# Seven block products (Strassen) for the projections of a delta-rule layer in batches two to four

## The chip, the core and the metric

The kernel runs on one core of a Trainium2 chip. The time is device microseconds of one execution: 3435.01 us is the median of three runs (3433.98 to 3443.59).

## What is computed

A decoder layer in float32 on x of 4 sequences by 512 tokens by 512 channels. Three blocks follow each other, each added to x: a gated delta-rule attention, a cross attention, and an ordinary attention with a mixture of experts. The change touches the first. It has 16 heads with keys and values of 128 channels:

```python
q = _causal_conv(x @ Wq.T, cw_q, cb_q)      # 4 taps, then SiLU
k = _causal_conv(x @ Wk.T, cw_k, cb_k)
v = _causal_conv(x @ Wv.T, cw_v, cb_v)
g = exp(-exp(A_log) * softplus(x @ Wa.T + dt_bias)); beta = sigmoid(x @ Wb.T)
q, k = l2norm(q), l2norm(k)
# per token t and head: S is a 128 x 128 state
error = v_t - g_t * (S k_t)
S = g_t * S + k_t (beta_t * error)^T
o_t = S^T q_t
o = rmsnorm(o) * norm_w * silu(x @ Wg.T)
return o @ Wo.T
```

## The kernel before

**Tiling.** Tokens of a sequence are worked in four chunks of 128 (TB = 4). A *pair* m is two neighbouring heads of one sequence: b = m // 8 is the sequence (called batch), hg = m % 8 the two heads; there are 32 pairs. Four projections belong to a pair, numbered n = 0 (q), 1 (k), 2 (v), 3 (gate g); one projection of one pair, 256 outputs by 512 channels by 512 tokens, is called a *unit* here. `conv` (L569 to L593) makes half a unit, one head: four matmuls of 128x128 weights by 512 tokens into a PSUM bank (L578; in the trace each float32 matmul counts as two passes), then for g a SiLU from PSUM, else the convolution: a scaled copy on ACT (L586), three multiply-adds on DVE that read the projection from PSUM (L589), and a SiLU on ACT (L592). The weights of a unit (512 KB) are loaded by `load_weights` into one buffer for each n, once its last user is done.

**Stages of a pair.** `stage1(m)` makes k for both heads, its transposes (L621) and their copy (L623), the sums of squares (ACT L626, clipped on DVE L632), their inverse roots by a power on POOL (L633), and from these the factors `ee` (L635), `ke` and `nr`; then the decay matrices `em`, spread by a scan on DVE (L642) and scaled by `ee` on ACT (`scale`, L438, four instructions per head), the k-k products (L651), then q, its product with k (`product`, 666), the decayed keys (`decayed`) and the sums of q's squares (`pss`, L698). `stage2_inverse(m)` inverts 32x32 diagonal blocks on POOL (L731, L732) and sends them through DRAM as T and X. `stage2_values(m)` makes v, transposes it (L779), multiplies it by `nr` (DVE, L781), and makes the gate. `stage3(m)` joins the blocks to full inverses (py L827 and L850, px L837 and L859, copies on ACT), and then runs the recurrence over the four chunks: for each head r (matmul L879, DVE L881), u (matmul L888, ACT L890), the new state (matmul L898, DVE L903) and the outputs into two banks `po` (L906, L908). `output(m)` multiplies by Wo (L952) and adds into the rows of x on DVE (L957).

**Order.** The stages are Python generators. `turns` mixes them: for each step of `stage3(m)` two steps of `stage1(m + 2)`, one of `stage2_values(m + 1)`, one of the inversion and one of `output(m - 1)`. ACT, DVE and POOL execute in exactly this written order (`manual_schedule`); for PE and for SP, which issues most transfers, a scheduler chooses the order when the kernel is built. Each engine then executes in order: an instruction that waits holds all behind it on its engine. A DMA that SP issues waits in SP's queue until its buffer is free.

**PSUM.** Eight banks of 128x512: four called `pb` (`p_b`) for everything wide, two called `ps` (`p_s`), each holding one 128x128 result of the recurrence at a time, two called `po`.

Of the kernel before, what the change touches and what calls it, by code (L numbers as in the profile page):

```python
# [31 lines left out]
F32 = mybir.dt.float32  # L32
BF16 = mybir.dt.bfloat16
AF = mybir.ActivationFunctionType
ALU = mybir.AluOpType
# [27 lines left out]
C_UP, C_LO, C_ONE, C_ID4, C_INV, N_TAB_A = 0, 1, 2, 3, 7, 7 + 8 // GRP  # L63
# [3 lines left out]
def _tables():  # L67
    ta, t = np.zeros((P, N_TAB_A, P), np.float32), np.zeros((P, N_TAB, P), np.float32)
    r, c = np.arange(P)[:, None], np.arange(P)[None, :]
    t[:, C_ID] = r == c  # L70
    ta[:, C_UP] = r <= c
    ta[:, C_LO] = r > c
    ta[:, C_ONE] = 1.0


    eye = np.eye(32, dtype=np.float32).reshape(32, 32 // GRP, GRP).transpose(2, 0, 1)
    ta[: GRP * 32, C_INV : C_INV + 8 // GRP] = eye.repeat(32, axis=0).reshape(GRP * 32, 8 // GRP, P)
    ta[:, C_ID4 : C_ID4 + 4] = (r == c)[:, None, :]
    t[:, C_CAUSAL] = np.where(c <= r, 0.0, MASKED)
    inv = (np.float32(1.0) / np.float32(1e6) ** (np.arange(0, RD, 2, dtype=np.float32) / np.float32(RD))).astype(np.float32)  # L80
    ang = (np.arange(S, dtype=np.float32)[:, None] * inv[None, :]).astype(np.float32)
    cos, sin = np.cos(ang), np.sin(ang)
    rope = np.concatenate([cos, cos, -sin, sin], axis=1).reshape(TB, P, P)
    t[:, C_ROPE : C_ROPE + TB] = rope.transpose(1, 0, 2)
    t[:, C_RANK, :NE] = np.arange(NE, 0, -1)
    t[:, C_RANK, NE : 2 * NE] = np.arange(NE) * B * S
    t[:, C_RANK, 16 : 16 + NT] = c[:, :NT] * P + r
    t[:, C_RANK, 32:96] = np.arange(64)
    t[:, C_BEFORE] = r < c
    t[:, C_ONES] = 1.0  # L90

    n = NE * (B * S + P) // P
    rows = np.zeros((P, n, 2), np.float32)
    rows[:, :, 0] = B * S + (np.arange(P * n) % P).reshape(P, n)
    t[:, C_LIST:].reshape(P, -1)[:, : 2 * n] = rows.reshape(P, 2 * n)
    return ta, t
# [8 lines left out]
def decoder(ctx: ExitStack, tc: tile.TileContext, a: dict, out: bass.AP):  # L105
# [21 lines left out]
    def rsqrt(dst, src, pool, add=0.0, mul=1.0):  # L127

        n = src.shape[1]
        t = pool.tile([P, 64], F32, name="rsq")  # L130
        nc.vector.tensor_scalar(t[:, :n], src, mul, add, ALU.mult, ALU.add)  # L131
        nc.gpsimd.tensor_tensor(dst, t[:, :n], mhalf[:, :n], ALU.pow)  # L132
# [233 lines left out]
    with ExitStack() as st:  # L366
# [10 lines left out]
        p_b = st.enter_context(tc.tile_pool(name="a_pb", bufs=4, space=PSUM))  # L377
        p_s = st.enter_context(tc.tile_pool(name="a_ps", bufs=2, space=PSUM))
        p_o = st.enter_context(tc.tile_pool(name="a_po", bufs=1, space=PSUM))

        tab_a = keep.tile([P, C_INV, P], F32, name="tab_a")
        nc.scalar.dma_start(tab_a, a["a_tables"][:, 0:C_INV, :])
        id4 = tab_a[:, C_ID4 : C_ID4 + 4, :].rearrange("p a b -> p (a b)")
# [21 lines left out]
        r_d = [dram.tile([HG * TB, P], F32, name=f"r_d{n}") for n in range(SLOTS)]  # L405

# [25 lines left out]
        def chunks(t):  # L432
            return t.rearrange("p c j -> p (c j)")
# [15 lines left out]
        def prologue(b):  # L449
# [18 lines left out]
            for c in range(TB):  # L468
                t = x[c]
                run(norms_of[c])  # L470
                if b:
                    yield
                    if c + 1 < TB:
                        next(norms_of[c + 1])
                    yield
                if c == 0:
                    xnT = s2.tile([P, KD, S], F32, name="xnT", bufs=2)
                    seqs[b] = [xnT]
                tp = p_b.tile([P, KD, P], F32, name="pb")
                for kd in range(KD):  # L480
                    nc.tensor.transpose(tp[:, kd, :], t[:, kd * P : (kd + 1) * P], ident)
                nc.scalar.copy(xnT[:, :, c * P : (c + 1) * P], tp)
                if b > 0 and c + 2 < TB:
                    load(c + 2)
                    norms_of.append(layernorm(x[c + 2].unsqueeze(1), x[c + 2].unsqueeze(1), small))
                yield
# [6 lines left out]
            yield  # L493
            pab = p_b.tile([P, TB, 32], F32, name="pb")
            for c in range(TB):
                nc.tensor.matmul(pab[:, c, :], quarters[:, c * P : (c + 1) * P], fold, start=True, stop=True)
            g_a, lg, beta, gam, ngam, gend, gall = (seq.tile([P, H1, TB], F32, name=n) for n in ("g_a", "lg", "beta", "gam", "ngam", "gend", "gall"))
# [63 lines left out]

        weights = {}

        def load_weights(m, *what, by=nc.sync):

            for n in what:
                if m < B * NHG:
                    t = (s1 if n < 2 else s2).tile([P, KD, HG * P], F32, name=f"w{n}", bufs=1)
                    by.dma_start(t, a["a_w"][m % NHG][:, n])  # L569
                    weights[m, n] = t  # L570
# [24 lines left out]
        keys, pairs = {}, {}  # L595

        def stage1(m):
# [3 lines left out]
            wk, wq = weights.pop((m, 1)), weights.pop((m, 0))  # L601

            def rows(n):
                t = s1.tile([P, HG, S], F32, name=f"row{n}", bufs=1)
                nc.sync.dma_start(chunks(t), g_d[b, n, hg * HG * TB : (hg + 1) * HG * TB].rearrange("c t -> (c t)").partition_broadcast(P))
                return [t[:, p, :] for p in range(HG)]

            kT, kt = [], []
            ss = small.tile([P, HG * TB], F32, name="ss", bufs=2)
            for p in range(HG):  # L610
                t = live.tile([P, S], F32, name="kT")
                yield from conv(b, hg, p, 1, wk, t)
                kT.append(t)
                yield
            xnT, beta, gam, ngam, gend, gall = seqs[b]
            gb = rows(0)
            load_weights(m + 1, 1)
# [21 lines left out]
            for p in range(HG):  # L639

                e = s1.tile([P, TB, P], F32, name="em")
                nc.vector.tensor_tensor_scan(chunks(e), gb[p], id4, 0.0, ALU.mult, ALU.add)  # L642
                em.append(e)
                yield
# [15 lines left out]
            qh, qg, pt, sq, kd_ = [], [], [], [], []  # L660

            def product(p):
# [4 lines left out]
                t = live.tile([P, TB, P], F32, name="pt", bufs=6)  # L667
                nc.vector.tensor_tensor(t, pq, em[p], ALU.mult)
                pt.append(t)

# [5 lines left out]
            for p in range(HG):  # L676
                q = s1.tile([P, S], F32, name="qh")
                c = conv(b, hg, p, 0, wq, q)
                yield from itertools.islice(c, 2)
                if p:  # L680
                    product(0)
                yield from c
                qh.append(q)
                g = live.tile([P, S], F32, name="qg", bufs=6)
                nc.gpsimd.tensor_tensor(g, q, mb[p], ALU.mult)  # L685
                qg.append(g)
                t = w2.tile([P, S], F32, name="cv", bufs=5)
                nc.scalar.activation(t, q, AF.Square)
                sq.append(t)
                yield  # L690
            load_weights(m + 1, 0)
            decayed(0)
            yield
# [11 lines left out]
            yield  # L705
            product(1)
# [3 lines left out]
            keys[m] = (kT, kd_, qg, pt, nr, rq)  # L710
# [57 lines left out]
        def stage2_values(m):  # L768
# [3 lines left out]
            wv, wg = weights.pop((m, 2)), weights.pop((m, 3))  # L772
            v_, gs = [], []
            for p in range(HG):
                t = yield from conv(b, hg, p, 2, wv, None)
                yield
                tp = p_b.tile([P, TB, P], F32, name="pb")
                for c in range(TB):
                    nc.tensor.transpose(tp[:, c, :], t[:, c * P : (c + 1) * P], ident)  # L779
                v = w2.tile([P, TB, P], F32, name="vn", bufs=4)  # L780
                nc.vector.tensor_tensor(v, tp, along(nr[:, p * TB : (p + 1) * TB], P), ALU.mult)  # L781
                v_.append(v)
# [5 lines left out]
            load_weights(m + 1, 2)  # L788
            for p in range(HG):
                g = w2.tile([P, S], F32, name="gs", bufs=3)  # L790
                yield from conv(b, hg, p, 3, wg, g)
                gs.append(g)
            load_weights(m + 1, 3)
# [19 lines left out]
        def stage3(m):  # L813
# [56 lines left out]
            for c in range(TB):  # L870
                cs = slice(c * P, (c + 1) * P)
                rs = []
                for p in range(HG):
# [4 lines left out]
                    pk = p_s.tile([P, P], F32, name="ps")  # L878
# [7 lines left out]
                for p in range(HG):  # L886
                    pu = p_s.tile([P, P], F32, name="ps")
# [6 lines left out]
                for p in range(HG):  # L894
                    h = hg * HG + p
                    if c < TB - 1:
                        pn = p_s.tile([P, P], F32, name="ps")
# [81 lines left out]
        def prepare():  # L979
# [4 lines left out]
            wk = [live.tile([P, S], F32, name="qg", bufs=6) for _ in range(2)]  # L984
            wk += [chunks(live.tile([P, TB, P], F32, name="pt", bufs=6)) for _ in range(2)]
# [66 lines left out]
        load_weights(0, 1, 0, 2, 3, by=nc.scalar)  # L1052
# [6 lines left out]
        run(itertools.islice(start, TB + 1))  # L1059
        pair0 = stage1(0)  # L1060
# [5 lines left out]
        for m in range(NP):  # L1066
            rest, turn = [], [0]
            if m == NP - 2:
# [5 lines left out]
                x_kT = x_keep.tile([P, 3, KD, M], BF16, name="x_kT")  # L1074
                nc.sync.dma_start(x_kT, x_kT_d)
# [3 lines left out]
            if m == NP - 1:  # L1079
                second.close()  # L1080
                v_keep = top.enter_context(tc.tile_pool(name="v_keep", bufs=1, side="right", reuse_waits="tile"))
                wpj = v_keep.tile([P, KD, D], F32, name="wpj")
# [22 lines left out]
            rest = turns(*rest)  # L1105
            for _ in stage3(m):
                next(rest, None)
            turn.clear()
# [631 lines left out]
```

## Time and profile before

| | |
|---|---|
| median of three runs | 3435.01 us (3433.98 to 3443.59) |
| profiled execution | 3435.95 us |
| its span | 3434.2 us |
| mean granted clock of TensorE | 0.978 |
| delta stage | 0 to some 1880 us |
| POOL power L633 | 32 times, 2438 ns each |
| DVE addition of 128x256 from PSUM (L1297) | 424 ns |
| DVE addition of 128x512 from PSUM (L957) | 689 ns |
| POOL multiplication of 128x512 (L685) | 1283 ns |

PE is TensorE's matmul queue, PEld its weight loads, which run beside it, DVE VectorE, ACT ScalarE, POOL GpSimd, SP the engine that issues DMAs. A group's row names line, engine, operation, output and inputs, shapes and count, and then busy time, mean nanoseconds of one instruction, and the idle time of the engine just before such instructions with what ended it. Matmuls are pipelined, so the mean of one (0.603 us for 512 columns) is longer than the distance from one to the next. A timeline row gives start and length in microseconds of a run of equal instructions, and in brackets the wait before it and what it waited for. Windows give the busy time of each engine in a stretch of the span. The granted clock is the share of full speed that TensorE was allowed.

### The profile page before, as it was taken

Reading aid. Unit: us, or ns where it says so; the run is one execution under the profiler, and the core shown is the slowest. Engines: PE = TensorE matmul, PEld = TensorE weight load, DVE = VectorE, ACT = ScalarE, POOL = GpSimd, SP = SyncE. Lnnn points to the kernel's source line nnn. Section 1 sums busy time; section 2 is a strip of 40 time slices with the busy share of each in tenths; the row PEclk is TensorE's granted clock in tenths of the full one; section 3 lists DMA queues with packets and bytes.
Section 4 is the critical chain, followed back from the end, with each engine's and each line's share of the span. In section 5 each row is a group of like instructions: output and inputs, shape, how many; then the busy total and the mean of one; then the engine's idle time right before and its main releaser. Section 6 shows DMA issues by size and latency. Waiting matters only on the chain. (4 is left out here: it accounts for less than half of the span.)

```text
span 3434.2 us, 49083 instructions
## 1 busy us (share of the span) xinstructions
PE 3253.7 (95%) x16596; PEld 1815.8 (53%) x16596; DVE 1836.7 (53%) x4155; ACT 1600.1 (47%) x4336; POOL 1449.6 (42%) x2766
## 2 busy tenths in 40 slices
PE   5899999999999999999997899999999999999996
PEld 2455555555555555555554455555555545554443
DVE  5755565555645556555545566656655665655111
ACT  3445555455554555455534345455454545534121
POOL 1156766667566675766752211121112111212442
PEclk7999999999999999999998899999999999999998
DMA  6343434534445343453432654445445544546444
GB/s 172 111 124 110 135 110 123 162 110 130 112 122 157 117 134 110 123 151 114 131 103 68 226 181 158 144 159 186 152 142 164 167 153 145 159 165 221 90 83 95
DMA packets 462250, 473.97 MB, mean 138 GB/s; under 512 B 199199, under 2 KB 310821, under 8 KB 461808
## 3 DMA queue, kind: packets, MB, share of 16 engines
q1 hardware_dynamic: 448656, 440.66, 42.2%
q0 software_dynamic: 11904, 27.34, 3.9%
q8 instruction: 132, 2.16, 0.3%
q10 hardware_dynamic: 1440, 2.84, 0.3%
q14 instruction: 118, 0.97, 0.1%
HBM read 410.15 MB, written 64.81 MB: 138 GB/s over the span
## 5 line engine op out<-in xcount | busy, mean ns | idle before, releaser
L578 PE MATMUL pb<-xnT,w 128*128 128x512 f32 x2048 | 959.4, 603 | 0.1
L578 PEld LDWEIGHTS pb<-xnT,w 128*128 128x128 f32 x2048 | 364.3, 192 | 337.4 <-issue 330.9
L589 DVE SCALAR_TENSOR_TENSOR cv<-pb,pp,cv 128x510 f32<-128x510 f32 (+2 forms) x576 | 424.3, 746 | 99.0 <-ACT cv L586 85.7
L732 POOL TENSOR_TENSOR iT<-iT,iW 64x126 f32<-64x126 f32 (+22 forms) x930 | 345.6, 372 | 72.8
L1229 PE MATMUL pb<-c_q,hT 128*128 128x512 f32 x768 | 362.9, 611 | 2.9 <-DMA c_q<-in_c_wk_dram 2.7
L731 POOL TENSOR_TENSOR iW<-iA,iT 64x126 f32<-64x126 f32 (+22 forms) x930 | 320.2, 344 | 65.8 <-issue 0.2
L952 PE MATMUL pb<-wot,og 128*128 128x512 f32 x512 | 246.0, 604 | 6.4 <-DVE xa L957 4.3
L1153 POOL TENSOR_TENSOR rope_s<-q,tab 128x128 f32<-128x128 f32 x64 | 36.6, 572 | 461.2 <-DVE q L1259 403.4
L1229 PEld LDWEIGHTS pb<-c_q,hT 128*128 128x128 f32 x768 | 144.6, 197 | 157.2 <-issue 153.5
L586 ACT ACTIVATE cv<-pb,pp 128x512 f32<-128x512 f32 x192 | 148.7, 774 | 147.5 <-PE pb L578 143.6
L633 POOL TENSOR_TENSOR rk<-ss,mhalf 128x8 f32<-128x8 f32 x32 | 78.0, 2438 | 277.3 <-DVE ss L632 277.3
L957 DVE TENSOR_TENSOR xa<-pb,xa 128x512 f32<-128x512 f32 x112 | 77.1, 689 | 189.8 <-PE pb L952 189.7
L1325 PE MATMUL po<-eT,val 128*128 128x512 f32 x320 | 167.2, 619 | 11.6 <-ACT eT L1323 8.6
L295 ACT ACTIVATE x_e<-pb,nm,x_step 128x256 f32<-128x256 f32 x256 | 141.2, 563 | 75.5 <-DVE nm L291 68.0
L1295 PE MATMUL pb<-kT,qT 128*128 128x256 f32 (+3 forms) x576 | 166.5, 416 | 0.7 <-ACT og L1301 0.6
L1335 PE MATMUL pw<-wot,oT 128*128 128x512 f32 x344 | 163.5, 602 | 0.4 <-DVE oT L1327 0.2
L685 POOL TENSOR_TENSOR qg<-qh,row 128x512 f32<-128x512 f32 x64 | 82.1, 1283 | 176.7 <-ACT qh L592 153.9
L952 PEld LDWEIGHTS pb<-wot,og 128*128 128x128 f32 x512 | 92.2, 191 | 101.8 <-issue 88.9
L1630 PE MATMUL pb<-w_gu,eT 128*128 x312 | 142.1, 599 | 2.0 <-issue 2.0
L1323 ACT COPY eT<-pb 128x512 f32<-128x512 f32 x160 | 90.8, 594 | 107.1 <-PE pb L1321 106.8
L592 ACT ACTIVATE qh<-cv 128x512 f32<-128x512 f32 x64 | 40.3, 630 | 213.0 <-DVE cv L589 205.1
L132 POOL TENSOR_TENSOR rms_r<-rsq,mhalf 128x1 f32<-128x1 f32 x48 | 27.4, 571 | 245.1 <-DVE rsq L131 245.0
(390 smaller groups left out, 6216.6 us busy)
## 6 DMA issues: line engine op xcount, KB each, us to landing
c_q<-in_c_wq_dram SPq DMA_DIRECT2D x128, 512.0 KB
w<-in_a_w_dram SPq DMA_DIRECT2D x124, 512.0 KB
wot<-in_c_wo_dram SPq DMA_DIRECT2D x86, 512.0 KB
row<-g_d SPq DMA_DIRECT2D x64, 512.0 KB
c_o<-in_c_wo_dram SPq DMA_DIRECT2D x42, 512.0 KB
at_d<-at SPq DMA_DIRECT2D x64, 256.0 KB
T<-t_d SPq DMA_DIRECT2D x32, 512.0 KB
X<-x_d SPq DMA_DIRECT2D x32, 512.0 KB
```

Source lines behind the costliest of these rows:

```text
L295: nc.scalar.activation(e[:, 2 * r + g, :], ps[r][:, g, :], AF.Exp, bias=nm[:, r, g : g + 1], scale=step[:, h : h + 1], accum_out=ssum[:, g ...
L578: nc.tensor.matmul(pj, wt[:, kd, p * P : (p + 1) * P], xnT[:, kd, :], start=kd == 0, stop=kd == KD - 1)
L586: nc.scalar.activation(ac, pj, AF.Identity, bias=cb[:, m, h : h + 1], scale=cw[:, m, h, 3:4])
L589: nc.vector.scalar_tensor_tensor(ac[:, j:], pj[:, : S - j], cw[:, m, h, 3 - j : 4 - j], ac[:, j:], ALU.mult, ALU.add)
L731: eng.tensor_tensor(u, A[:, i, i + 1 :].unsqueeze(2).to_broadcast([nb, n, w]), T[:, i, :w].unsqueeze(1).to_broadcast([nb, n, w]), ALU.mult)
L732: eng.tensor_tensor(T[:, i + 1 :, :w], T[:, i + 1 :, :w], u, ALU.add)
L952: nc.tensor.matmul(pw, og[p][:, c * P : (c + 1) * P], wot[:, p, :], start=p == 0, stop=p == HG - 1)
L1229: nc.tensor.matmul(pj, hT[:, kd, :], w[:, kd % 2, :], start=kd == 0, stop=kd == KD - 1)
L1295: nc.tensor.matmul(ps[:, m, k * P : (k + w) * P], qT[g][:, n + m, :], kT[:, g, j : j + w, :], start=True, stop=True)
L1325: nc.tensor.matmul(po, val[:, g, :], eT, start=k == 0, stop=k == c)
L1335: nc.tensor.matmul(pw, oT[:, h + m, :], w[:, m, :], start=g == 0 and h + m == 0, stop=g == 3 and h + m == 3)
L1630: nc.tensor.matmul(pg, hT[:, kd, :], w_gu[:, bass.ds(e, 1), kd, :, :], start=kd == 0, stop=kd == KD - 1)
```

## The change

For pairs of the first sequence (m < 8) a unit is projected as before. From m = 8 on it is made as a 2x2 block product by Strassen's method in the form with seven products: halves of the outputs (the two heads), of the channels and of the tokens. A product is two matmuls of 128x128 weights by 256 tokens, so 14 of 256 columns stand in place of 8 of 512. Their results are added on DVE into SBUF (`plus`), and the convolution then reads SBUF. A unit is now finished for both heads before its convolution begins (`seven`, `convs`).

```diff
+        def seven(b, n, wt, dst):
+            x = moving[b]
+            def products(*ns):
+                ps = p_b.tile([P, 2, S // 2], F32, name="pb")
+                for k, n in enumerate(ns):
+                    w, v = x[n]
+                    for kd in range(2):
+                        nc.tensor.matmul(ps[:, k], wt[:, w, kd, :], v[:, kd, :], start=kd == 0, stop=kd == 1)
+                return ps[:, 0], ps[:, 1]
...
+            l, r = products(0, 4)
+            nc.scalar.copy(c11, l)
+            plus(c12, c11, r)
+            yield
+            l, r = products(5, 2)
+            plus(c21, c12, l)
+            plus(c22, c21, r)
+            plus(c12, c12, r)
+            yield
+            l, r = products(1, 3)
+            plus(c11, c11, l)
+            plus(c21, c21, r)
+            yield
+            l, _ = products(6)
+            plus(c12, c12, l)
+            yield
```

The four sums of weight blocks that a unit needs are made once, while the first sequence uses the same weights plainly (`combine`: four additions of 128x256, on POOL for the first six units, on DVE for the rest), stored to DRAM (`used`), and read back with the plain blocks by the later sequences (`load`). Weight buffers are now three in turn for all units, filled three units ahead. The sums of x's blocks are four subtractions on POOL per sequence (`differences`).

```diff
+        def combine(u):
+            if u[0] < NHG:
+                t = summed[u] = s1.tile([P, 3, 2, S // 2], F32, name="xd", bufs=1)...
+                eng = nc.gpsimd if u in order[:6] else nc.vector
+                for dst, x, y, op in ((t3, a11, a21, ALU.subtract), ...):
+                    eng.tensor_tensor(dst, x, y, op)
...
+            if m < NHG:
+                nc.sync.dma_start(sums_d[m % NHG, n], summed.pop((m, n)))
+            if i + 1 < len(order):
+                combine(order[i + 1])
+            weights.pop((m, n))
+            load()
```

PSUM is divided anew: five banks for `pb`, one for the recurrence, whose four quarters are used in turn.

```diff
-        p_b = st.enter_context(tc.tile_pool(name="a_pb", bufs=4, space=PSUM))
-        p_s = st.enter_context(tc.tile_pool(name="a_ps", bufs=2, space=PSUM))
+        p_b = st.enter_context(tc.tile_pool(name="a_pb", bufs=5, space=PSUM))
+        p_s = st.enter_context(tc.tile_pool(name="a_ps", bufs=1, space=PSUM))
+        quarters_ = p_s.tile([P, 4, P], F32, name="ps")
+        quarter = itertools.cycle([quarters_[:, n, :] for n in range(4)])
...
-                    pk = p_s.tile([P, P], F32, name="ps")
+                    pk = next(quarter)
```

Around it, orders and buffers change. In `stage2_values` both heads of v are projected and convolved, then both are transposed; the multiplication by `nr` goes from DVE to four scalings on ACT per head. In `stage1` both squares of q come together, before `product(0)`, and the scan of `em` is done in four pieces:

```diff
-                v = w2.tile([P, TB, P], F32, name="vn", bufs=4)
-                nc.vector.tensor_tensor(v, tp, along(nr[:, p * TB : (p + 1) * TB], P), ALU.mult)
+                scale(v_[p], tp, nr, p)
...
-                nc.vector.tensor_tensor_scan(chunks(e), gb[p], id4, 0.0, ALU.mult, ALU.add)
+                for c in range(TB):
+                    nc.vector.tensor_tensor_scan(e[:, c, :], gb[p][:, c * P : (c + 1) * P], ident, 0.0, ALU.mult, ALU.add)
...
+                square(0)
+                square(1)
+                yield
+                yield
+                product(0)
```

To make room in SBUF, qh and qg share a tile (the decay is multiplied in place), `pt` has five buffers for six (so `product(1)` and `decayed(1)` of the next pair but one wait in the written order until `stage3` of this one is through: `while busy: yield`), the two `row` tiles become one, the table `id4` goes, some small tiles shrink, and one load of the cross attention (`x_kT`) moves to the last pair.

## The prediction

> **What bounds the kernel now.** The table of busy time first: TensorE is busy for 95% of the span, nobody else for over 53%.
>
> ```profile
> PE 3253.7 (95%) x16596; PEld 1815.8 (53%) x16596; DVE 1836.7 (53%) x4155; ACT 1600.1 (47%) x4336; POOL 1449.6 (42%) x2766
> ```
>
> An average says nothing of the stage that is changed, so next the windows of the delta stage (columns: length, then busy time and count of PE, PEld, DVE, ACT, POOL, then granted clock, DMA share, GB/s), here a slice of a middle batch and the first one of the batch after it:
>
> ```profile
> 1140.00:1200.00 60.00, 59.74 (x342) 34.96 (x341) 32.51 (x53) 30.34 (x88) 41.73 (x91) 1.00 0.43 124
> 1260.00:1320.00 60.00, 56.78 (x344) 33.35 (x343) 35.44 (x76) 35.87 (x93) 36.25 (x78) 1.00 0.42 117
> ```
>
> PE is full at full clock; a pair takes 52.8 us (L837 of one pair starts at 1172.39, of the next at 1225.18). So PE work removed here is worth its time, as long as PE then waits for nothing. Whether it will is read from the one chain per pair that is long already, in the timeline (start, length, instructions, and in brackets the wait before):
>
> ```profile
> 1027.11 0.66 PE L779 MATMUL pb<-tab,cv 128*128 128x128 f32 x4
> 1032.44 1.95 PE L651 MATMUL pb<-kT 128*128 128x128 f32 x16
> 1034.23 1.88 PE L578 MATMUL pb<-xnT,w 128*128 128x512 f32 x4
> 1035.95 0.61 PE L888 MATMUL ps<-r,X 128*128 128x128 f32 x4
> 1036.39 3.60 PE L578 MATMUL pb<-xnT,w 128*128 128x512 f32 x8
> ```
>
> ```profile
> 1031.49 0.19 ACT L626 ACTIVATION_READ_ACCUMULATOR pb<-pb 128x1 f32 x1
> 1035.05 2.44 ACT L438 ACTIVATE em<-em,ee 128x128 f32<-128x128 f32 x8 [3.04 <-POOL ee L635]
> ```
>
> ```profile
> 1032.04 2.42 POOL L633 TENSOR_TENSOR rk<-ss,mhalf 128x8 f32<-128x8 f32 x1 [7.66 <-DVE ss L632]
> ```
>
> ACT stands still for 3.04 us behind POOL's power (L633), as it does for every pair. It costs nothing, since PE has projections to run (L578 before and after L888), and since the transposes of v (L779) were through 5 us before. This cover is what the change touches.
>
> **PE work removed.** A logical matmul is two passes in the trace. Eight passes of L578 take 3.60 us, of which one whole pass is 0.603 (its row), so (3.60 - 0.603)/7 = 0.43 us from pass to pass; for 128 columns (1.95 - 0.279)/15 = 0.111. Straight between them 256 columns make 0.2155. A unit (256 outputs x 512 tokens) goes from 16 passes of 0.43 (6.90 us) to 28 of 0.2155 (6.03): 0.86 us less, 3.45 us for the four units of a pair, 82.8 us for the 24 pairs of batches two to four. From the other side, by busy time per pass:
>
> ```profile
> L578 PE MATMUL pb<-xnT,w 128*128 128x512 f32 x2048 | 959.4, 603 | 0.1
> L1295 PE MATMUL pb<-kT,qT 128*128 128x256 f32 x224 | 58.7, 387 | 0.0
> ```
>
> 959.4/2048 x 16 = 7.50 us against 58.7/224 x 28 = 7.34: only 0.16 us per unit, 15 us in all. A weight load (0.192, single) is below 0.2155, so it fits behind the pass, closely. I take 82.8, since these L1295 are short runs, and keep 15 for the range.
>
> **Other engines.** Each unit gains seven DVE additions of 128x256 from PSUM (0.42 each by the row of L1297) and an ACT copy. Per pair that is 28 x 0.42 = 11.8 us on DVE, less the v multiplications (two of 0.69) that go to ACT: DVE goes from some 29 us of 52.8 (32.51 of 60) to about 39, ACT from 27 to about 31 (four copies of 0.37, eight scalings of 0.31). Neither becomes the bound by its sum. The scan in four pieces adds under 1 us to DVE, POOL's differences (four per batch) and the loads one unit ahead (0.43 of the DMA is used) cost nothing while PE is the bound; if that cover goes they are still under 1 us per pair. What counts is order.
>
> **New waits, per pair.** I followed the changed kernel's order of instructions on PE and ACT through one pair of a later batch with the durations above.
>
> 1. *The transposes of v.* A unit is now finished for both heads before its convolutions start, so v's SiLU comes later in ACT's order: behind the four scalings `em` of the first head, thus behind POOL's power. On PE the two groups of four v transposes stand right behind the k-k products and four projections, and everything after waits with them, the recurrence's matmuls included. From the end of the last square of k: 3.56 us to `em` (1031.49 to 1035.05), four scalings 1.22 (half of 2.44), SiLU 0.63, release 0.1: 5.5 us. PE gets there about 0.4 us after that square, 1.5 at most if it is itself held up before. Stall 4.0 to 5.1; I take 4.4.
> 2. *One bank for four quarters.* The recurrence's tile "ps" is one tile now, and each matmul into a quarter waits for the reader of the previous one. A round of r, u or state for two heads was two matmuls side by side and their readers; it is now matmul, reader, matmul, reader. Where a projection stands between, nothing is lost. After the second px none does: a matmul with its latency (0.45) and a copy (0.65), 1.1 us, and 0.35 for the release: 1.4. The third and fourth rounds lose about 0.7 together. From the other side: all four rounds filled, 0; none filled, 8 readers of 0.6, 4.8.
> 3. *The tail of a pair.* Both squares of q now come together, ahead of the sums `pss`, which wait 0.95 us for them on PE, and the last u/u and r/r alternate without a projection between them: 0.45 + 0.65 + 0.45. Together 2.5 us, where before PE had L578 there:
>
> ```profile
> 1216.30 0.61 PE L888 MATMUL ps<-r,X 128*128 128x128 f32 x4
> 1216.74 1.88 PE L578 MATMUL pb<-xnT,w 128*128 128x512 f32 x4
> 1218.46 0.39 PE L906 MATMUL po<-pt,u 128*128 128x128 f32 x2
> ```
>
> Less the 0.3 that this tail loses today: 2.2.
>
> 4.4 + 1.4 + 0.7 + 2.2 = 8.7 us of stalls against 3.45 saved: +5.2 per pair, 58.0 instead of 52.8. Over the 23 pairs that run all of it: **+120 us**.
>
> **The clock.** A wait of this size shows in this trace what it costs besides, at the end of the delta stage (windows; length, PE busy, granted clock, DMA share, GB/s):
>
> ```profile
> 1783.00:1787.00 4.00, 0.75 (x4) 1.00 0.37 49
> 1787.00:1791.00 4.00, 1.45 (x7) 0.66 0.61 165
> 1791.00:1795.00 4.00, 4.00 (x11) 0.50 0.47 114
> 1795.00:1799.00 4.00, 4.00 (x22) 0.99 0.02 4
> ```
>
> ```profile
> 1789.55 0.79 PE L888 MATMUL ps<-r,X 128*128 128x128 f32 x2 [4.88 <-DVE r L881]
> ```
>
> After 4.88 us without work the clock is 0.5 until about 1795: some 5.4 us at half speed, 2.7 us of work lost. For stalls of 4.0 to 5.1 this is 0 to 2.7 per pair, 0 to 62 us; part falls into later waits, which shorten by it. I take a third: **+20**. The Trainium skill's "TensorE: Matmul & The Clock Gate" (table of clock states) puts the fall to half clock at an idle window of some 3.4 us; by it every pair would pay and the sum would be 40 higher, by a reading in which only gaps like 4.88 count, 20 lower.
>
> **First batch and start.** Pairs of the first batch keep their projections and gain only the waits of one bank (1.4) and, on DVE and ACT, the weight sums (4 of 0.42 per unit) and a 512 KB store whose single buffer holds the next sums back: 1 to 2 us for five pairs, **+8** (0 to 15). Before 180 us PE is idle for some 53 us and each step is a chain; eight sums on POOL at some 0.75 (half of L685's 1.28 for twice the size, and a store) stand ahead of the first power: **+6** (0 to 10).
>
> **Sum**, against the profiled execution (3435.95, of which 3434.2 is the span; 0.94 above the median): 3436 + 120 + 20 + 8 + 6 = **3590**.
>
> **Rivals.**
>
> *B, the stalls are covered: faster.* Place: the v transposes. If what PE has before them is 4 us longer than I count, because products or projections ahead of them wait for DVE's additions or for a bank, or ACT gets v's SiLU out ahead of `em`, the 4.4 vanishes; with the half of the rest that projections could fill, 2 us remain against 3.45. Then 23 x -1.5 = -35, and with no stall at all -83, plus 14 at the start: 3370 to 3415. For it speaks that the same engine order keeps PE at 59.74 of 60 us today; against it that ACT's order is fixed by the code, and that the 3.56 us are in every pair. It decides at the SiLU of v: under 1 us of stall there, and the saving wins.
>
> *C, only the first stall is there,* the rounds with one bank being filled: 4.4 - 3.45 = +1 per pair, with start and clock 23 + 14 + 20: 3490. For it: projections stand between most rounds.
>
> *D, the passes save nothing.* With 15 us in place of 82.8 the stalls of A come on top: 3655. Only short runs speak for it.
>
> The rows of L888 show four recurrence passes back to back into two banks today (0.61 us). The Trainium skill's "PSUM — Partial Sum Buffer" (PSUM bank collisions) calls two engines at one bank and one group of 32 partitions at a time an error, even at different columns; no row here shows it. By it the waits of step 2 are no accident of how the tile is declared, and four separate tiles in that bank would need them too; the sum stays.
>
> **Chances.** A (3530 to 3640) 0.56, B 0.22, C 0.16, D 0.06. The range leaves out the faster half of B and the end of D: 3400 to 3650; A's own is 3530 to 3640. A measurement of this kernel tells some 0.3% (10 us) from no change: faster 0.21, same 0.05, slower 0.74.
>
> **What would show it.** Right: in a pair of the second to fourth batch, PE's wait of 4 to 5 us ahead of the v transposes, released by ACT; ACT's wait behind `ee`; clock below 1.00 in such slices; a pair of 58 us; 28 passes with a pitch of 0.22. Wrong: PE again at 59 of 60 us, a pair near 50; or stalls elsewhere, above all behind DVE's additions, which I hold for covered (39 of 58 us).

## The result, and the profile after

| | before | after |
|---|---|---|
| median | 3435.24 us (4 runs, 3433.98 to 3443.59) | 3723.19 us (4 runs, 3717.28 to 3730.10) |
| ratio | | 1.0833 (95%: 1.0804 to 1.0862) |
| span of the profiled execution | 3434.2 us | 3715.2 us |
| mean granted clock | 0.978 | 0.949 |
| an ordinary pair of batches two to four | 52.8 us | 60.2 to 65.1 us |
| a pair of the first batch | 52.8 us | 55.4 to 56.8 us |

Slower, as forecast, by 288 us where 155 were forecast; the range ended at 3650. A pair is the time from one second px (L859, now L987) to the next.

The page's table of busy time, and of its groups the row of the new products:

```profile
PE 3322.9 (89%) x17748; PEld 2132.0 (57%) x17748; DVE 2120.1 (57%) x5059; ACT 1695.0 (46%) x4688; POOL 1548.7 (42%) x2802
...
L637 PE MATMUL pb<-xnT,w 128*128 128x256 f32 x1536 | 418.0, 399 | 1.4 <-ACT pb L754 1.4
```

PE is busy for longer although it has less to do, and idle for 392 us where it was for 181. Both are seen in windows (columns as in the prediction: PE, PEld, DVE, ACT, POOL, clock, DMA share, GB/s):

```profile
1140.00:1260.00 120.00, 103.57 (x649) 81.71 (x645) 74.49 (x150) 53.23 (x158) 69.39 (x138) 0.91 0.52 145
1260.00:1380.00 120.00, 104.37 (x684) 82.27 (x684) 74.27 (x150) 59.26 (x178) 74.22 (x149) 0.96 0.47 131
```

PE works 104 of 120 us, and at 0.91 to 0.96 of its clock. What ended its waits in the later batches (480 to 2080 us; total, times, longest):

```profile
PE pb L913 <- ACT cv L702: 96.7, 23, 4.7
PE pb L832 <- ACT cv L794: 36.3, 21, 2.5
PE ps L1016 <- ACT u L1018: 30.4, 70, 5.8
PE ps L1026 <- DVE state L1031: 11.7, 2, 6.0
PE ps L1016 <- DVE r L1009: 11.5, 26, 0.4
PE ps L1007 <- DVE r L1009: 6.0, 17, 1.0
```

The first row is the wait ahead of v's transposes (L913), once in each of 23 pairs, 4.2 us each, ended by v's SiLU (L702); in the kernel before, the same waits (L779) add up to 0.9 us (480 to 1780 us). The second are the sums of q's squares (L832), the others the rounds of the recurrence in one bank (the two of 6 us at L1026 fall in pairs that carry the next sequence's prologue on DVE as well). One pair's timeline shows the chain, on POOL, ACT and PE:

```profile
777.46 1.65 POOL L761 TENSOR_TENSOR rk<-ss,mhalf 128x8 f32<-128x8 f32 x1 [10.72 <-DVE ss L760]
...
780.11 1.28 ACT L441 ACTIVATE em<-em,ee 128x128 f32<-128x128 f32 x4 [2.30 <-POOL ee L763]
781.30 1.13 ACT L702 ACTIVATE cv<-cv 128x512 f32<-128x512 f32 x2
...
776.72 1.03 PE L637 MATMUL pb<-xd,w 128*128 128x256 f32 x4
781.97 1.12 PE L913 MATMUL pb<-tab,cv 128*128 128x128 f32 x4 [4.22 <-ACT cv L702]
782.87 1.91 PE L637 MATMUL pb<-xd,w 128*128 128x256 f32 x4
```

Four passes of a product take 1.03 us before the wait and 1.91 after it. The windows of 4 us around it say why (columns as above):

```profile
777.00:781.00 4.00, 0.74 (x4) 0.31 (x2) 3.78 (x9) 1.70 (x6) 3.31 (x5) 0.86 0.00 0
781.00:785.00 4.00, 3.04 (x10) 2.68 (x11) 0.06 (x1) 1.43 (x4) 3.20 (x11) 0.50 0.00 0
785.00:789.00 4.00, 3.65 (x20) 3.01 (x19) 2.21 (x6) 1.30 (x5) 3.61 (x6) 0.79 0.24 42
789.00:793.00 4.00, 4.00 (x25) 3.56 (x25) 2.93 (x8) 2.84 (x11) 1.90 (x7) 1.00 0.78 222
```

The clock falls within the wait and is back at about 787 us. Summed as busy time x (1 - clock) over windows of 4 us, PE loses 80 us to it in the 23 intervals from the px at 509 us to that at 1983 us, and 88 us from 480 to 2080 us; before, in the same intervals, none. Of the 80, 47 us are lost around v's waits. The rest lies mostly behind shorter waits, such as this one for q's squares

```profile
864.11 0.43 PE L832 MATMUL pb<-cv,tab_a 128*32 128x128 f32 x8 [1.70 <-ACT cv L794]
```

and the window of 4 us behind it:

```profile
865.00:869.00 4.00, 3.54 (x20) 2.46 (x18) 1.76 (x6) 0.00 (x0) 3.29 (x10) 0.57 0.24 71
```

And the tail of the pair, where r and u take turns in one bank:

```profile
803.32 0.43 PE L832 MATMUL pb<-cv,tab_a 128*32 128x128 f32 x8 [1.73 <-ACT cv L794]
...
806.05 0.49 PE L1007 MATMUL ps<-state,kT 128*128 128x128 f32 x2 [0.22 <-DVE r L1009]
806.98 0.49 PE L1016 MATMUL ps<-r,X 128*128 128x128 f32 x2 [0.44 <-DVE r L1009]
807.82 0.49 PE L1016 MATMUL ps<-r,X 128*128 128x128 f32 x2 [0.35 <-ACT u L1018]
```

From 806.05 a matmul (two passes of 0.11 us each) starts only every 0.84 to 0.93 us. Starts compared with the pitches (0.43, 0.2155 and 0.111 us per pass) give for this pair 48.0 us of work and 13.6 of waiting and slow clock (before: 51.3 and 1.5): 4.4 at v's transposes, 2.3 by half clock behind them, 2.2 in the first rounds of the recurrence, 4.2 in the tail, 0.5 elsewhere.

### The profile page after: what moved, and what is told of

The parts are those of the page before. It is cut to its first block, busy times and chain, and to the rows that moved or that the text cites. A ratio compares the mean times of both kernels' runs of the same rounds, so it can differ in the third digit from the quotient of the medians.

```text
span 3715.2 us, 53179 instructions
## 1 busy us (share of the span) xinstructions
PE 3322.9 (89%) x17748; PEld 2132.0 (57%) x17748; DVE 2120.1 (57%) x5059; ACT 1695.0 (46%) x4688; POOL 1548.7 (42%) x2802
## 5 line engine op out<-in xcount | busy, mean ns | idle before, releaser
L867 POOL TENSOR_TENSOR iW<-iA,iT 64x126 f32<-64x126 f32 (+22 forms) x930 | 355.8, 383 | 214.5 <-DMA iA<-at_d 137.8
L637 PE MATMUL pb<-xnT,w 128*128 128x256 f32 x1536 | 418.0, 399 | 1.4 <-ACT pb L754 1.4
L868 POOL TENSOR_TENSOR iT<-iT,iW 64x126 f32<-64x126 f32 (+22 forms) x930 | 378.4, 407 | 73.0 <-POOL iW L867 0.2
L637 PE MATMUL pb<-xd,w 128*128 128x256 f32 x1152 | 305.8, 392 | 0.0
L712 PE MATMUL pb<-xnT,w 128*128 128x512 f32 x512 | 250.5, 619 | 5.8 <-DVE at L783 5.8
L637 PEld LDWEIGHTS pb<-xd,w 128*128 128x128 f32 x1152 | 221.6, 197 | 28.6
L1018 ACT COPY u<-ps 128x128 f32<-128x128 f32 x256 | 67.9, 265 | 360.8 <-PE ps L1016 360.6
L1009 DVE SCALAR_TENSOR_TENSOR r<-ps,ngam,vn 128x128 f32<-128x128 f32 x192 | 66.7, 348 | 155.2 <-PE ps L1007 155.1
L696 DVE SCALAR_TENSOR_TENSOR cv<-vn,pp,cv 128x511 f32<-128x511 f32 x144 | 107.6, 747 | 82.9 <-ACT cv L694 79.5
L696 DVE SCALAR_TENSOR_TENSOR cv<-qg,pp,cv 128x511 f32<-128x511 f32 x144 | 125.4, 871 | 25.0 <-ACT cv L694 20.7
```

The costliest lines, as they stand in the source:

```text
L637: nc.tensor.matmul(ps[:, k], wt[:, w, kd, :], v[:, kd, :], start=kd == 0, stop=kd == 1)
L696: nc.vector.scalar_tensor_tensor(ac[:, j:], dst[p][:, : S - j], cw[:, n, h, 3 - j : 4 - j], ac[:, j:], ALU.mult, ALU.add)
L712: nc.tensor.matmul(pj, wt[:, kd, p * P : (p + 1) * P], xnT[:, kd, :], start=kd == 0, stop=kd == KD - 1)
L867: eng.tensor_tensor(u, A[:, i, i + 1 :].unsqueeze(2).to_broadcast([nb, n, w]), T[:, i, :w].unsqueeze(1).to_broadcast([nb, n, w]), ALU.mult)
L868: eng.tensor_tensor(T[:, i + 1 :, :w], T[:, i + 1 :, :w], u, ALU.add)
```

## The experiments

Times are medians; the kernel before, measured beside them, took 3430.8 to 3436.8 us. Sums of waits are PE's, over the later batches; the clock's loss is that of the same 23 intervals in each kernel, summed as above; line numbers are those of each kernel.

**e1: v's first SiLU ahead of em on ACT.** PE's order stays almost as it was.

```diff
+                res.append(ac)
+                if n == 2 and p == 1:
+                    nc.scalar.activation(res[0], res[0], AF.Silu)
                 yield
...
-                res.append(ac)
-            for p in range(HG):
+            for p in range(n == 2, HG):
                 nc.scalar.activation(res[p] if n == 2 else dst[p], res[p], AF.Silu)
```

> The changed kernel with one edit in ACT's order: in the later batches the SiLU of v's first head is issued right after the convolution of the second head is issued, ahead of the four scalings of em, not behind them. Theory 1 (the wait before the v transposes is ACT's order behind POOL's power, and the half clock that follows it is its consequence): the wait of 4.2 us falls below 1, the windows of 4 us stay at clock 1.00, and a pair of 61.6 us loses 3.5 for the wait and some 2.3 for the clock: 56 us, in all 23 x 5.5 = 125 less, near 3595 us. Theory 2 (PE would only meet the next late thing, the second head's SiLU or r, so that the wait moves): 61 us per pair, 3690 to 3720.

3644.63 us, ratio 1.062 (1.0593 to 1.0646): 78 less. The waits:

```profile
PE ps L1009 <- DVE r L1011: 23.3, 46, 2.7
...
PE pb L957 <- DMA T<-t_d: 17.3, 12, 2.2
PE pb L915 <- ACT cv L699: 14.4, 21, 1.1
```

The wait at v's transposes (L915) fell from 96.7 to 14.4 us, so its cause was ACT's order, as theory 1 has it. Of the 82 us, 17 came back at r (6.0 before) and 16 at T, the inverse from POOL (1.6 before), and the clock's loss fell only from 80 to 49 us. Theory 2 holds for that part.

**e2: two banks for the recurrence, four for products.**

```diff
-        p_b = st.enter_context(tc.tile_pool(name="a_pb", bufs=5, space=PSUM))
-        p_s = st.enter_context(tc.tile_pool(name="a_ps", bufs=1, space=PSUM))
+        p_b = st.enter_context(tc.tile_pool(name="a_pb", bufs=4, space=PSUM))
+        p_s = st.enter_context(tc.tile_pool(name="a_ps", bufs=2, space=PSUM))
...
-                    pk = next(quarter)
+                    pk = p_s.tile([P, P], F32, name="ps")
...
```

> The changed kernel with the old division of PSUM alone: four banks for pb, and two for the recurrence, one 128x128 result each. Theory 1 (one bank makes each round of r, u and state wait for a reader in the middle, where no projection stands between): the pairs of the first batch lose 2 us, those of the later batches 2 to 3.5 us, the wait before the v transposes stays at 4.2: 3630 to 3670 us. Theory 2 (the rounds were covered, and the fifth bank for products is what keeps the additions off PE's path): 3720 or more.

3593.87 us, ratio 1.0472 (1.0445 to 1.05): 130 less, more than either theory had. A pair of the first batch takes 54.4 us, an ordinary later one 57.0 to 60.1. The waits for u and r in the bank are gone, and with them the one for q's squares (36.3 us before); that for T, the inverse, came up (24.3 us). The scheduler also chose another order for PE here (a matmul of u, for one, now stands ahead of the sums of q's squares), so the 130 us are the bank together with that order. What stays first is

```profile
PE pb L911 <- ACT cv L700: 74.6, 23, 3.6
```

3.2 us in each of 23 pairs, and the clock still loses 57 us. The fifth bank for products was worth less than the second one for the recurrence.

**e4: plain projections in all batches,** one bank kept. Weight sums are made and not read.

```diff
-                if m < NHG:
+                if True:
...
             res = []
-            if m < NHG:
+            if True:
...
```

> The changed kernel with plain projections for all 32 pairs; the weight sums of the first batch are still made and stored, and nothing reads them; the differences of x are left out. One bank, the order of squares, the scan in pieces, three weight buffers and the scaling of v on ACT stay. Theory 1 (most of the loss sits in the path of the products, above all that v is finished for both heads before its SiLU): pairs like those of the first batch now, 55 to 57 us, less in later ones without sums: 3500 to 3560 us. Theory 2 (the loss is in the rearrangement around them): 3650 or more.

3497.65 us, ratio 1.0193 (1.0167 to 1.0218): theory 1. A later pair takes 54.0 us: without products no wait at v's transposes is left.

**e5: the kernel before, with one bank.**

```diff
+        quarters_ = p_s.tile([P, 4, P], F32, name="ps")
+        quarter = itertools.cycle([quarters_[:, n, :] for n in range(4)])
...
-                    pk = p_s.tile([P, P], F32, name="ps")
+                    pk = next(quarter)
...
```

> The kernel before with the new division of PSUM alone: five banks for pb, and one bank in four quarters for the recurrence. Theory 1 (a reader between any two matmuls of a round costs time even beside plain projections): 1.5 to 3 us per pair, 3480 to 3530 us. Theory 2 (projections of 512 columns between the rounds cover it): under 3450 us.

3525.85 us, ratio 1.0281 (1.0256 to 1.0307): theory 1. 55.6 us per pair instead of 52.8: one bank costs 2.8 us per pair even with plain projections between the rounds.

**e6: both edits, e1 and e2.**

> Both edits at once: v's first SiLU ahead of em, and the old division of PSUM. They took 78 and 130 us each. Theory 1 (two causes at different places of a pair): the gains add, 3480 to 3520 us, a pair near 53.5 us, with the clock at 1.00 in it. Theory 2 (both shorten the same wait, the r and u of the pair's start): 3560 or more.

3614.12 us, ratio 1.0531 (1.0508 to 1.0553): 20 more than with two banks alone. The time lies in theory 2's range, but neither theory holds: the wait for v went, and two other waits came up:

```profile
PE pb L955 <- DMA T<-t_d: 68.5, 22, 5.5
PE ps L1016 <- DVE r L1009: 46.0, 24, 3.0
```

T, the inverted blocks, is now 3 us late in 22 pairs, and r stands behind v's second convolution on DVE.

**e7: the wait filled with needless matmuls.**

```diff
                 tp = p_b.tile([P, TB, P], F32, name="pb")
+                if p == 0 and m >= NHG:
+                    for _ in range(14):
+                        nc.tensor.matmul(tp[:, 0, :], ident, ident, start=True, stop=True)
```

> The changed kernel with 14 needless 128x128 matmuls (28 passes of 0.11 us, 3.1 us of PE work) written into the bank of v's transposes just ahead of them, in the later batches: the wait of 4.2 us is filled with work, and nothing behind it can start earlier. Theory 1 (after the wait TensorE runs at half clock for some microseconds, 2.3 us per pair lost): the windows after it stay at 1.00, a pair loses 2 us, 23 x 2 = 46 less: 3665 to 3690 us. Theory 2 (the lower clock in the records costs nothing that the wait itself does not cost): 3720 or more, by what the fillers add.

3642.96 us, ratio 1.0619 (1.0596 to 1.0642): 80 less, with 3 us more work per pair, and more than theory 1 had. Behind the filled waits the clock stays at 1.00 in every pair but the last: the 47 us lost there are the 46 of theory 1. The clock's loss fell further, from 80 to 23 us, since PE's order shifted (r's matmuls ahead of v's transposes) and the wait for q's squares went as well (36.3 to 3.2 us), while T's came up (29 us). What each of these is worth by itself was not tried.

**e8: no weight sums.**

```diff
-            if m < NHG:
-                nc.sync.dma_start(sums_d[m % NHG, n], summed.pop((m, n)))
-            if i + 1 < len(order):
-                combine(order[i + 1])
...
```

> The changed kernel without its weight sums: no additions of weights and no stores in the first batch; the later batches load as many bytes from the plain weights in their place, so their projections are of wrong weights, in the same time. Theory 1 (sums on DVE and POOL, and the one buffer that waits for the store, cost the first batch some 2 us per pair and the start 5 to 9): 3695 to 3712 us, a pair of the first batch 54.5 instead of 56.8. Theory 2 (they lie beside PE's work): within 6 us of 3723.

3696.44 us: 27 less, theory 1. A pair of the first batch takes 54.0 us instead of 55.4 to 56.8, the first interval 62.7 instead of 67.4.

**e9: e6 with its steps aligned as before the change.** The second scan's yield goes in later batches, and v's second convolution comes a step later:

```diff
                 em.append(e)
-                yield
+                if p == 0 or m < NHG:
+                    yield
...
+                elif p == 0:
+                    nc.scalar.activation(ac, ac, AF.Silu)
+                    yield
```

> The kernel of both edits (e6), with its steps aligned as they were before the change: in the later batches both heads' em come in one step of the recurrence, ahead of u on ACT (one yield less after the second scan), and v's second convolution one step later, behind r on DVE. In e6 PE waited 68 us for T from the inversion and 46 us for r. Theory 1 (both waits are order again: the k-k products reach the inversion 3 us later than they could, and r stands behind a convolution of 2.3 us): both go, with the half clock after them, 23 x 5 to 6 us: 3475 to 3510 us. Theory 2 (POOL, DVE or the copies of u are the next bound, whatever the order): 3560 or more.

3546.84 us, ratio 1.0327 (1.0293 to 1.036): 67 less than e6, between the theories. The wait for r went, T kept 43.5 us. SP's queue shows why:

```profile
802.21 1.54 SPq L786 DMA_DIRECT2D at_d<-at  x2
809.95 0.33 SPq L920 DMA_DIRECT2D r_d<-rq  x1
810.39 0.98 SPq L858 DMA_DIRECT2D iA<-at_d  x2
```

The loads of the blocks to invert (L858) stand behind a store of `rq`, which waits for a power on POOL that ends at 809.93 us.

**e10: that power and store in the middle of v's products.**

```diff
+            made = convs(m, 2, [chunks(v) for v in v_])
+            if m >= NHG:
+                yield from itertools.islice(made, 4)
+                roots()
+            ts = yield from made
...
```

> The kernel of e9 with one more order changed: in the later batches POOL's power for q's norms and its store to DRAM are issued in the middle of v's products, not after v's first transposes. In e9 that store stood on SP for POOL's power at 809.95 us, ahead of the loads of the inversion's blocks, and PE waited 43 us for T. Theory 1 (SP's order holds the inversion back): the wait for T goes, 1.8 us per pair and part of the half clock: 3485 to 3510 us. Theory 2 (the inversion is late on POOL itself, 83 of 120 us busy): within 10 us of e9's 3547.

3487.69 us, ratio 1.0168 (1.0151 to 1.0185): 59 less than e9, theory 1. In SP's queue the loads now follow the stores of `at` after 4 us, and the wait for T is gone:

```profile
789.17 1.54 SPq L786 DMA_DIRECT2D at_d<-at  x2
793.24 0.93 SPq L858 DMA_DIRECT2D iA<-at_d  x2
```

An ordinary pair takes 53.4 us, though its PE work is 48 us: order, with the bank, was most of the loss, and not all of it.

**e11: plain projections and two banks** (e4 and e2 together).

> Plain projections for all 32 pairs (as e4) with the old division of PSUM (as e2): what is left of the change is the weight sums in the first batch, which nothing reads, and the buffers and orders around them. Theory 1 (one bank is what cost e4's pairs 54.0 us instead of 52.8): 52.8 us per later pair, 3450 to 3470 us, the rest being sums and start (27 us in e8). Theory 2 (scan in pieces, v's scaling on ACT and one row tile cost on their own): 3480 or more.

3436.63 us, ratio 1.0022 (1.0008 to 1.0035), better than theory 1: 52.4 us per later pair. The buffers and orders around the products together cost next to nothing (the first batch, with its weight sums, is longer, and the later pairs are shorter). Beside e4, the second bank is worth 1.6 us per later pair.

**e12: e11 without the weight sums.**

> Plain projections for all 32 pairs, the old division of PSUM, and no weight sums: of the change only the buffers and orders around the products are left (three weight buffers in turn, v's scaling on ACT, the scan in pieces, fewer tables and tiles). In e11 a later pair took 52.4 us, where the kernel before takes 52.8. Theory 1 (these orders gain a little, and the sums of the first batch hid it): 3410 to 3425 us, faster than the kernel before. Theory 2 (pairs of the first batch take 54 us without sums too): 3430 or more.

3422.16 us, ratio 0.9965 (0.9952 to 0.9979), theory 1: faster than the kernel before, by 0.35%, 52.4 us per pair from the first batch on. It is what the change would give with its products left out, and the fastest kernel here. Which of its edits gains the 0.4 us was not tried.

**e13: e10 with k's squares read from SBUF.**

```diff
-                    nc.scalar.activation(tp[:, c, :], tp[:, c, :], AF.Square, accum_out=ss[:, p * TB + c : p * TB + c + 1])
+                    nc.scalar.activation(e[:, c, :], t[:, c, :], AF.Square, accum_out=ss[:, p * TB + c : p * TB + c + 1])
```

> The kernel of e10 with the squares of k read from its copy in SBUF and written to the later em tile, so that the bank of k's transposes is free after the copy and not 1.8 us later; in e10 a product waited 0.65 us for it in every pair. Theory 1 (with four banks, products wait for banks): 0.6 to 0.8 us per pair, 3470 to 3478 us, still over the kernel before. Theory 2 (the next product waits for the banks of the k-k products instead): within 6 us of e10's 3488.

3487.45 us, ratio 1.0152 (1.0139 to 1.0165): theory 2; an ordinary pair takes 53.2 us instead of 53.4. The wait for the squares' bank went (14.9 us in e10), and those for banks that DVE reads grew from 17 to 23 us (`at`, made of the k-k products) and from 5 to 12 us (`qg`, the sums of q's products).

## Why the prediction was wrong

The direction and the chain at v's transposes were right; the terms for the clock, the tail and the first batch were too small, and one pair was left out.

- **PE work removed: right.** Eight passes of a product take 1.89 us and four 1.03, so 0.215 from pass to pass; a pair's work fell by 3.4 us (3.45 forecast). "Straight between" 0.111 and 0.43 would be 0.217; the 0.2155 that I used is half of 0.431.
- **The transposes of v: right**, in place, cause (e1) and size: 96.7/23 = 4.2 us against 4.4. Some of the size is luck: POOL's power took 1.65 us where I counted with 2.42, the multiplication behind it 0.61 where I had 0.20, and PE came some 0.4 us later.
- **One bank, first rounds: right in the pair read**, 2.2 us against 2.1.
- **The tail of a pair: too small.** 4.2 us in place of 2.2. I counted the wait for q's squares (1.73 in the pair read, 0.95 forecast) and one alternation; there are four matmuls with a reader between each two. In e2 these waits are gone.
- **The clock: the step that failed.** "I take a third: +20": it is 80 us in the 23 intervals. Each of the 23 waits of v comes with half clock, within it or just behind it, and not a third of them; that makes 47 us (my own bound was 62). The other 33 us I had put at nothing, since I priced no other wait. In e2, with 3.2 us at the same place, the clock still falls at 20 of 23 waits, and in the changed kernel within 3.4 us behind 11 of 21 waits for q's squares, which are 0.9 to 2.5 us long.
- **First batch and start: 30 us where I had 8, and 5 us shorter where I had 6 longer.** The six intervals of the first batch are 30 us longer and the start 5 shorter: 25 in place of 14. Without the weight sums (e8) the six are 15 us shorter, so half of the 30 is the sums.
- **Left out:** the next to last interval (v and g of the last pair as products), 16 us longer.

Together, in the spans: 154 forecast and 281 measured; 237 instead of 140 in the 23 intervals, of which the clock makes 60 and the tail 1.7 x 23 = 39 (2 too many, as one pair read stands for all), 16 for the pair left out, 11 for the start, 3 after the delta stage.

What makes the clock fall can be worked out from the traces. Their records of the clock hold a value for 3.41 us or a multiple of it. I counted how much of each such step PE's passes fill, each pass as long as its pitch (1 ns per column for those under 128 columns), in all 14 traces from 480 to 1780 us. The 185 falls to half clock follow steps that are filled by 0.41 at most; of the 4866 full-clock steps that no fall follows, the least filled has 0.37. The wait of 1.70 us at 864.11 lies in a step filled by 0.37, and the clock falls; that of 1.73 us at 803.32 lies in one filled by 0.42, and it does not. So in these runs it is not the length of one wait that counts, but how little PE does in some 3.4 us. The Trainium skill's "TensorE: Matmul & The Clock Gate" (table of clock states) has the fall after an idle window of some 3.4 us; the length agrees with the steps here, but the step need not be idle.

Rivals B and C would have needed a covered wait; D was wrong, passes cost what their pitch says. B's rule (under 1 us of stall at v's SiLU, and the saving wins) did not hold: in e1 the stall is 0.65 us and the time 6% above the kernel before. B's thought that in a better order the saving wins is answered by e10 and e11, for the orders tried: with the same banks a pair with products takes 53.4 us and a plain one 52.4, though it has 3.4 us less work on PE. PE's largest waits in e10 are for a bank: 17.2 us until DVE has multiplied the k-k products into `at`, 14.9 us for k's squares on ACT, and 4.9 us until DVE has added q's products. So the additions, which I held for covered, are a small part; in the pair read (`at` at 735.15 us) DVE stood idle for 0.71 us for ACT's `em`.

## What to carry to other kernels

Work taken from the bounding engine is worth its time only if what it now meets is on time: follow the new order of every engine and of the DMA queue for one period. When one wait is taken away, expect the next in the chain, and price each by its wait plus the clock that is lost behind it. A wait shorter than 3 us can cost the clock too, if PE does little around it. Buffers that readers of different engines share, here one bank for four results, can cost even where work stands between (2.8 us per pair in e5).

## What the runs showed that I had not expected

POOL's power of 128x8 takes 2.44 us on average where DVE runs the scan in whole rows beside it (the kernel before and e5), and 1.67 us in every kernel of these with the scan in four pieces (after, e10, e11). The kernel before has a second power of the same size (L785, for q's norms) with no scan beside it, and its mean there is 1.67 us too. The first power and the scans beside it:

```profile
707.18 2.33 DVE L642 TENSOR_TENSOR_SCAN em<-row,tab_a 128x512 f32<-128x512 f32 x2
707.42 2.42 POOL L633 TENSOR_TENSOR rk<-ss,mhalf 128x8 f32<-128x8 f32 x1 [7.66 <-DVE ss L632]
```

So the scan in whole rows costs the power 0.8 us. One scan takes 1.2 us, and the first was 0.24 us old when the power started; a piece in the changed kernel takes 0.4 us. The delay fits a power that cannot begin its work until the scan then running has ended. The Trainium skill's "SBUF — State Buffer" (Terms, shared port pair) has DVE and GpSimd take a port in turns, each for a whole instruction. The start agrees with that; the rest does not: in the changed kernel further pieces of the scan run inside the power's 1.65 us (from 777.46) and still take 0.40 us each, no longer than others. It stays argued: the scan alone was not changed.

And one bank for four results cost 2.8 us per pair beside plain projections in the old order (e5) and 1.6 in the new one (e4 against e11: 54.0 and 52.4), where I had put 1.4 for the pairs of the first batch.
